# A four-layer graph network on one core: a store tied to a later sum, and second neighbour lists in layer 2

## The chip, the cores and the metric

The kernel runs on one core of a Trainium2 chip. The metric is device time in microseconds of one execution, the median over several. The engines are TensorE (PE, with its weight loads as PEld), VectorE (DVE), ScalarE (ACT), GpSimd (POOL) and SyncE (SP). SP and POOL issue DMAs, which 16 DMA engines carry out.

## The reference

A graph of 2708 nodes has a weighted adjacency matrix `adj` (symmetric in pattern, float32) and 512 features a node. Low-numbered nodes have many neighbours, high-numbered ones few. Four pre-norm layers follow one another; each adds its output to `x`:

```python
# layer 0: incidence
mask = adj > 0
head = mask / sqrt(sum(mask, -1))
inc = adj + head
x = x + (inc @ h) / sum(inc, -1)          # h = relu(layernorm(x))
# layer 1: attention, 8 heads, masked with adj
atts = q @ k.T / sqrt(64) - 1e16 * (1 - max(adj, I))
x = x + softmax(atts) @ v @ Wo
# layer 2: two graph convolutions
h = relu(adj @ (h @ W1) + b1)             # pass 1
h = relu(adj @ (h @ W3) + b3)             # pass 2
x = x + tanh(h @ Wf + bf)
# layer 3: mean over neighbours
A = (adj != 0)
x = x + (A @ (h @ W + b)) / sum(A, 0)
```

## The kernel before

The nodes are cut into 22 tiles of 128 (the last has 20). A row tile `m` is a block of 128 outputs; its product with the adjacency matrix is a sum over column tiles. Since the matrix is sparse, only the first six column tiles (`DENSE` = 6, 768 nodes) are multiplied as dense blocks. For the other columns each row tile has a list of the nodes that are a neighbour of any of its 128 nodes, in chunks of 128:

```python
CHUNKS = (0, 10, 9, 8, 7, 7, 7, 7, 6, 6, 6, 6, 6, 6, 6, 5, 6, 5, 5, 5, 5, 2)
```

Row tile 0 has no list and multiplies all tiles. For a listed chunk the kernel gathers 128 rows of features and 128 rows of the row tile's adjacency columns by indirect DMAs on POOL, one gather each.

Layer 0 builds the lists while it computes (loop at L729). The adjacency rows of a tile are loaded (L473, `ar`); ACT and PE count the neighbours by column (`counts`, stored at L277), and for a group of three row tiles (`GROUP`) a running sum gives each column its rank in the list (`rank_blocks`, L314 to L321, which stores `rank_b`; `rank_rows` for row tiles 1 and 2, which stores `rank_l` at L342). `load_ranks` (L354, L360) spreads a row's ranks over the 128 partitions, and `search` (L363 on) finds the place of each rank with a find-index operation on DVE (L377) and writes the indices `idx_a` (for adjacency entries) and `idx_g` (for feature rows). POOL then gathers the adjacency entries `ac` (L532, three buffers) and the feature rows `h` (L550). `incidence(m)` builds `inc` from dense blocks `at` (loaded at L574) and `incl` from `ac` with two DVE operations each (`add_head`, L592 and L600), PE sums them into `acc` (L741), and `ac` itself is kept for later layers: its store to `listed[m]` (`lst`, L618) is put on the list `pending`, which `flush` issues from SP at the next turn of the loop. The rest of a turn belongs to layers 0 and 1: norm, transposes (L185), value projection (L157), the store of `y` (L695), loads of `x` (L701, L705).

Layer 2's pass 1 (loop at L1039) goes over row tiles 0 to 9, 21, 10 to 20. `aggregate` (L905) loads `ac` back (L890), gathers feature rows of the first product from `g1d` (L897) into eight places `gg0` to `gg7`, and loads the six dense column tiles in two pieces of three (`raw`, L880). The dense product is exact to float32 by three reduced-precision products of split operands: `a_hi` (ACT, L933), `a_lo` and `a_s` (DVE, L934 and L935), three matmuls for each column tile (L946). The listed chunks use float32 matmuls (L949, two records each in the profile). In pass 1 (`marked`) ACT also writes the sign of every block to `nz` (L915), which is stored for layer 3. Then come the bias (L974), relu and transposes (L837 to L846), the next projection (`project3`, L862), its sum `go` (L830, L831) and its store to `g2d` (L1048). All first products (L1009 to L1025, with stores to `x2` and to `g1d`) fall into the turn of row tile 0. Pass 2 (loop at L1208: row tiles 0, 6 to 9, 21, 10 to 20, 1 to 5) is the same without marks, with gathers from `g2d`. Layer 3 (L1133 and around) counts with the marks.

The program text gives an order of issue for each engine that is then rearranged: [...] So an added dependence can change where instructions of other engines stand. Buffers are given by name in pools with a set number of copies; [...]

Of the kernel before, what the change touches and what calls it, by code (L numbers as in the profile page):

```python
# [9 lines left out]
FP = mybir.dt.float32  # L10
FR = mybir.dt.float32r
BF = mybir.dt.bfloat16
HF = mybir.dt.float16
U32 = mybir.dt.uint32
# [3 lines left out]
ALU = mybir.AluOpType  # L18
# [4 lines left out]
P = 128  # L23
# [12 lines left out]

DENSE = 6
LEAD = 3
CHUNKS = (0, 10, 9, 8, 7, 7, 7, 7, 6, 6, 6, 6, 6, 6, 6, 5, 6, 5, 5, 5, 5, 2)


@with_exitstack
def kernel(
# [27 lines left out]
    nc = tc.nc  # L71
# [15 lines left out]
    def rows(t):  # L87
        return min(P, N - t * P)

    def dense_of(m):  # L90

        return 0 if m == NT - 1 else DENSE
# [33 lines left out]
    BEHIND = DENSE * P  # L126
    WIDE, LOW = (N - BEHIND) // 4, BEHIND // 2
    assert WIDE * 4 == N - BEHIND and WIDE < BLK and LOW * 2 == BEHIND
    cnt_b = dram.tile([NGROUP, P, WIDE], BF, name="cnt_b")
    cnt_l = dram.tile([NGROUP, P, LOW], BF, name="cnt_l")  # L130

# [2 lines left out]

    idx = const.tile([P, NT], U32, name="idx")
    BAD_BOUND, BAD_NEG, BAD_MANY = NT, NT + 1, 2 * NT + 1
    bad = const.tile([P, 3 * NT + 1], FP, name="bad")
    nc.gpsimd.memset(bad, 0.0)
    flag = const.tile([P, 1], I32, name="flag")

# [1 line left out]
    idx_g = const.tile([P, NT, NCH], U32, name="idx_g")  # L142

    rdeg = const.tile([P, NT], FP, name="rdeg")
    ones_b = const.tile([P, 1], BF, name="ones_b")
    nc.gpsimd.memset(ones_b, 1.0)

# [69 lines left out]
    with tc.tile_pool(name="l0_slab", bufs=2) as slabs, tc.tile_pool(  # L217
# [29 lines left out]
        nc.gpsimd.iota(place_i, pattern=[[P, NCH]], base=1, channel_multiplier=1)  # L247
        places = hp.tile([P, NCH], FP, name="places")
        nc.vector.tensor_copy(places, place_i)

        pending, pending_c = [], []

# [329 lines left out]
        def incidence(m):  # L582

            n = rows(m)
            rn = row[m][0]
            dg = wp.tile([P, P], FP, name="dg")
            nc.vector.tensor_scalar(dg[:n, :n], ident[:n, :n], rn[:n], None, op0=ALU.mult)
            rb = ps_small.tile([P, P], FP, name="rb")
            nc.tensor.matmul(rb[:, :n], ones[:n], dg[:n, :n], start=True, stop=True)

            def add_head(inc, a, k, num):
                nc.vector.scalar_tensor_tensor(  # L592
                    inc,
                    a,
                    0.0,
                    rb[:k, :n].unsqueeze(1).to_broadcast([k, num, n]),
                    op0=ALU.is_gt,
                    op1=ALU.mult,
                )
                nc.vector.tensor_tensor(inc, inc, a, ALU.add)  # L600

            pairs = []
            if m >= LEAD:
                pieces = [tiles_d] if dense_of(m) else []
            else:
                pieces = in_order if m + 1 < LEAD else dense_last
            for ts in pieces:
                if m == 0:
                    for t in ts:
                        h0_tile(t)  # L610
                at, k = blocks.pop(m) if m in blocks else load_block(m, ts)
                d = (slice(0, k), slice(0, len(ts)), slice(0, n))
                inc = slabs.tile([P, PIECE0, P], FP, name="inc", bufs=3)
                add_head(inc[d], at[d], k, len(ts))
                pairs += [(inc[:k, i, :n], h0[t][:k]) for i, t in enumerate(ts)]
            if m >= LEAD:
                ac, gs = gathers.pop(m)
                pending.append(lambda: nc.sync.dma_start(out=listed[m], in_=ac))  # L618
                inc = slabs.tile([P, NCL, P], FP, name="incl")[:, : CHUNKS[m], :n]
                add_head(inc, ac, P, CHUNKS[m])  # L620
                pairs += [(inc[:, c, :], g) for c, g in enumerate(gs)]
            return pairs

# [189 lines left out]
    NMARK = DENSE + NCA  # L813
    gather_slot = [0]

    def gathered():
        name = f"gg{gather_slot[0] % NGG}"
        gather_slot[0] += 1
        return gp.tile([P, D], FP, name=name)

    def sum_banks(dst, main, mixed, n):

# [54 lines left out]
    def load_piece(m, ts):  # L877
        n, k = rows(m), rows(ts[0])
        raw = ap.tile([P, PIECE, P], FP, name="raw", bufs=3)
        nc.sync.dma_start(  # L880
            out=raw[:k, : len(ts), :n],
            in_=adj_t[ts[0] * P : ts[0] * P + k * len(ts), m * P : m * P + n].rearrange(
                "(t p) m -> p t m", p=k
            ),
        )
        return raw[:k, : len(ts), :n], k

    def load_listed(m):
        ac = ap.tile([P, NCA, P], FP, name="ac")[:, : CHUNKS[m], : rows(m)]
        nc.sync.dma_start(out=ac, in_=listed[m])  # L890
        return ac

    def gather(m, gd, gs=None, index=idx_g):

# [10 lines left out]
    def aggregate(m, parts, shifted, gd, marked):  # L905
# [4 lines left out]
        if marked:  # L910
            nz = ap.tile([P, NMARK, P], U8, name="nz", bufs=3)

            def mark(i, a):
                k, ts = a.shape[:2]
                nc.scalar.activation(nz[:k, i : i + ts, :n], a, AF.Sign)  # L915
# [1 line left out]
        mixed = ps_a.tile([P, D], FP, name="aggs")  # L917
        chunks = []
        if num:
            ac = load_listed(m)  # L920
            chunks = [(ac[:, c, :], g) for c, g in enumerate(gather(m, gd))]
            if marked:
                mark(whole, ac)
        for ts in dense if dense_of(m) else []:
            gs = [parts(t) for t in ts]
            raw, k = load_piece(m, ts)
            hi, lo, s = (
                ap.tile([P, PIECE, P], FR, name=f"a_{part}") for part in ("hi", "lo", "s")
            )
            d = (slice(0, k), slice(0, len(ts)), slice(0, n))  # L930
            if marked:
                mark(ts[0], raw)
            nc.scalar.activation(hi[d], raw, AF.Copy, scale=UP)  # L933
            nc.vector.tensor_tensor(lo[d], raw, hi[d].bitcast(FP), ALU.subtract)  # L934
            nc.vector.scalar_tensor_tensor(  # L935
                s[d], lo[d].bitcast(FP), SHIFT, hi[d].bitcast(FP), op0=ALU.mult, op1=ALU.add
            )
            for i, t in enumerate(ts):
                ghi, glo, gs_ = gs[i]
                first, last = t == 0, t == DENSE - 1  # L940
                for acc, a, b, st, sp in (
                    (main, hi, ghi, first, False),
                    (main, lo, glo, False, last),
                    (mixed, s, gs_, first, False),
                ):
                    nc.tensor.matmul(acc[:n], a[:k, i, :n], b[:k], start=st, stop=sp)  # L946
# [89 lines left out]
    w3 = split_w(wsetb, wr, "wb")  # L1036
    wr = load_w(wset, wf_d, "wr")

    for m in order_m:  # L1039
        n = rows(m)  # L1040
        parts = aggregated(m, first_parts, first_product, g1d, bias1, marked=True)
        if m == 0:
            wf = split_w(wset, wr, "wa")
            wr = load_w(wset, w_d, "wr")
        main, mixed = project3(parts, n, w3)
        go = wp.tile([P, D], FP, name="go")
        sum_banks_scaled(go, main, mixed, n)
        nc.sync.dma_start(out=g2d[span(m)], in_=go[:n])  # L1048
# [158 lines left out]
    FIRST = 2  # L1207
    for m in order_2:  # L1208
        n = rows(m)
        parts = aggregated(m, second_parts, second_product, g2d, bias3)  # L1210
        if m == 0:
            w = split_w(wsetb, wr, "wb")
# [499 lines left out]
```

## Time and profile before

| | |
|---|---|
| median of 9 runs | 1521.31 us (1518.84 to 1529.21) |
| profiled execution | 1525.66 us, of which its span is 1523.9 us |
| mean granted TensorE clock | 0.935 |
| HBM traffic | 230 GB/s over the span |
| layer 0 | about 60 to 520 us |
| layer 2, pass 1 | 540 to 950 us, of which row tile 0 up to about 655 us |
| layer 2, pass 2 | 960 to 1280 us |
| layer 3 | from 1280 us |

Times within a trace count from the span's start. In lines of a timeline the first number is the start, the second the duration, both in us; square brackets give the idle time of that engine just before and what ended it. `SPq` is a DMA issue on SP's queue. A line of the waits view reads: who waited, for whom, us in total, times, longest. [...]

### The profile page before, as it was taken

To read this page: it belongs to the slowest core of one execution; us is meant where nothing else is said; L and a number is where in the kernel's file an instruction comes from. 1 tells how busy PE (TensorE), PEld (TensorE's weight loads), DVE (VectorE), ACT (ScalarE), POOL (GpSimd) and SP (SyncE) were. 2 spreads that over 40 slices of the span, in tenths; PEclk is the share of its full clock that TensorE was granted. 3 is DMA by queue.
4 is the path that set the end of the run, shared out by engine and by line. 5 is a ranking of instruction groups with operands and counts; after the bars stand their busy time and mean duration, and the time that the engine had idled before them with its cause. 6 is when DMAs were issued, how large, how long until landed. Compare 5 with 4: busy or idle time off the path is not lost.

```text
span 1523.9 us, 15398 instructions
## 1 busy us (share of the span) xinstructions
PE 1313.0 (86%) x4400; PEld 772.9 (51%) x4400; DVE 940.5 (62%) x1888; ACT 676.8 (44%) x1040; POOL 673.0 (44%) x690
## 2 busy tenths in 40 slices
PE   6487689789778669979999999899999998777887
PEld 2133234334333247645656665565667666565564
DVE  3568688878879579533344445555666655564654
ACT  5987375363111256422333334444454544444443
POOL 1264566666553321055544442243343444066653
PEclk9699989899889889999999999999999999798999
DMA  8999888987696687277777777655555656476864
GB/s 307 314 328 323 286 284 298 298 272 225 192 327 216 172 282 245 93 222 252 247 234 227 235 232 245 198 183 187 157 172 176 202 185 201 155 229 208 250 209 151
DMA packets 195940, 351.27 MB, mean 231 GB/s; under 512 B 26444, under 2 KB 107692, under 8 KB 192113
## 3 DMA queue, kind: packets, MB, share of 16 engines
q1 hardware_dynamic: 148453, 200.68, 39.6%
q0 software_dynamic: 47392, 149.51, 31.5%
q8 instruction: 37, 0.61, 0.2%
q14 instruction: 58, 0.48, 0.1%
HBM read 286.99 MB, written 63.12 MB: 230 GB/s over the span
## 4 chain that ended last, share of the span: by engine, by line
PE 51%; DMA 5%; DVE 3%; issue 3%; ACT 2%; another core or an unknown queue 2%; SPq 0%; ACTq 0%; POOLq 0%; DVEq 0%; POOL 0%
PE aggs L949 13%; PE main L862 9%; PE agg L946 7%; PE mixed L862 4%; PE agg L1133 4%; PE aggs L946 4%; PE aggs L1133 3%; PE pt L837 3%; DMA raw<-in_adj_t_dram 2%; PE agg L862 1%; PE aggs L961 1%; PE mixed L1133 1%; PE main L1133 1%; DMA ac<-lst 1%
## 5 line engine op out<-in xcount | busy, mean ns | idle before, releaser
L949 PE MATMUL aggs<-gg,ac 128*128 128x512 f32 (+1 forms) x520 | 232.4, 594 | 4.5 <-DMA gg<-g1d,idx_g 3.5
L897 POOL DMA_INDIRECT gg<-g2d,idx_g x130 | 131.0, 1008 | 223.0 <-PE aggs L949 173.4
L897 POOL DMA_INDIRECT gg<-g1d,idx_g x130 | 132.4, 1019 | 181.3 <-PE aggs L949 108.4
L741 PE MATMUL acc<-h,inc 128*128 128x512 f32 x348 | 166.8, 620 | 33.2 <-DVE inc L600 27.3
L532 POOL DMA_INDIRECT ac<-in_adj_t_dram,idx_a x130 | 130.2, 1002 | 78.4 <-issue 38.1
L550 POOL DMA_INDIRECT h<-h0d,idx_g x111 | 117.7, 1060 | 103.7 <-PE acc L741 70.4
L949 PEld LDWEIGHTS aggs<-gg,ac 128*128 128x128 f32 (+1 forms) x520 | 97.5, 189 | 111.3 <-issue 103.4
L741 PEld LDWEIGHTS acc<-h,inc 128*128 128x128 f32 x348 | 65.0, 196 | 111.7 <-issue 74.1
L933 ACT ACTIVATE a_hi<-raw 128x384 fp32r<-128x384 f32 x84 | 43.5, 520 | 168.8 <-issue 96.6
L946 PE MATMUL agg<-ghi,a_hi 128*128 128x512 f32 x252 | 115.1, 457 | 3.4 <-ACT a_hi L933 3.1
L946 PE MATMUL agg<-glo,a_lo 128*128 128x512 f32 x252 | 102.4, 406 | 4.1 <-ACT glo L200 4.1
L897 POOL DMA_INDIRECT gg<-hidr,idx_h x79 | 78.2, 990 | 58.0 <-PE agg L1133 20.6
L741 PE MATMUL acc<-h,incl 128*128 128x512 f32 (+1 forms) x222 | 103.2, 611 | 0.0
L946 PE MATMUL aggs<-gs,a_s 128*128 128x512 f32 x252 | 100.4, 401 | 0.7 <-DVE gs L197 0.6
L934 DVE TENSOR_TENSOR a_lo<-raw,a_hi 128x384 fp32r<-128x384 f32 x84 | 47.2, 562 | 85.0 <-ACT a_hi L933 48.5
L157 PE MATMUL yacc<-wvo,hT 128*128 128x512 f32 (+1 forms) x176 | 88.7, 650 | 8.8 <-ACT hT L186 5.2
L843 DVE SCALAR_TENSOR_TENSOR v_lo<-pt,v_hi 128x512 fp32r<-128x512 f32 (+1 forms) x88 | 56.9, 665 | 48.3 <-ACT v_hi L842 28.6
L824 DVE SCALAR_TENSOR_TENSOR u<-aggs,u 128x512 f32<-128x512 f32 x42 | 28.9, 687 | 79.2 <-PE aggs L949 57.8
L842 ACT ACTIVATE v_hi<-pt 128x512 fp32r<-128x512 f32 (+1 forms) x88 | 49.0, 578 | 47.7 <-PE pt L837 36.4
L483 ACT ACTIVATE sgn<-ar 128x2708 bf16<-128x2708 f32 (+1 forms) x22 | 54.0, 2455 | 34.1 <-DMA ar<-in_adj_dram 28.2
L741 PEld LDWEIGHTS acc<-h,incl 128*128 128x128 f32 (+1 forms) x222 | 42.7, 196 | 52.0 <-issue 51.3
L514 DVE FIND_INDEX8 at_top<-top,ar 128x8 uint32<-128x2708 f32 (+1 forms) x22 | 65.3, 2970 | 0.0
(275 smaller groups left out, 2785.0 us busy)
## 6 DMA issues: line engine op xcount, KB each, us to landing
ar<-in_adj_dram SPq DMA_DIRECT2D x27, 1354.0 KB
raw<-in_adj_t_dram SPq DMA_DIRECT2D x108, 192.0 KB
slot<-x SPq DMA_DIRECT2D x41, 256.0 KB
at<-in_adj_t_dram SPq DMA_DIRECT2D x27, 384.0 KB
ranks<-rank_b SPq DMA_DIRECT2D x20, 485.0 KB
ac<-lst SPq DMA_DIRECT2D x16, 384.0 KB
h<-in_x_dram SPq DMA_DIRECT2D x21, 256.0 KB
h0d<-h POOLq DMA_DIRECT2D x21, 256.0 KB
```

What stands on the lines that cost most here:

```text
L157: nc.tensor.matmul(acc[:n], hT[:, c, :n], w[:, c, :], start=(c == 0), stop=(c == NCD - 1))
L483: nc.scalar.activation(sgn[:n], ar[:n], AF.Sign, accum_out=sum_sgn[:n])
L514: nc.vector.max_index(at_top[:n], top[:n], ar[:n])
L532: nc.gpsimd.indirect_dma_start(out=ac[:, c, :n], out_offset=None, in_=adj_units, in_offset=bass.IndirectOffsetOnAxis(ap=idx_a[:, m, c0 + c ...
L550: nc.gpsimd.indirect_dma_start(out=g, out_offset=None, in_=h0d[:, :], in_offset=bass.IndirectOffsetOnAxis(ap=idx_g[:, m, c : c + 1], axis=0),)
L741: nc.tensor.matmul(acc[:n], a, g, start=(i == 0), stop=(i == len(pairs) - 1))
L843: nc.vector.scalar_tensor_tensor(lo[d], pt[d], 0.0, hi[d].bitcast(FP), op0=ALU.max, op1=ALU.subtract)
L862: nc.tensor.matmul(acc[:n], a[:, c, :n], b[:, c, :], start=first and c == 0, stop=last and c == NCD - 1,)
L897: nc.gpsimd.indirect_dma_start(out=gs[c], out_offset=None, in_=gd[:, :], in_offset=bass.IndirectOffsetOnAxis(ap=index[:, m, c : c + 1], ax ...
L946: nc.tensor.matmul(acc[:n], a[:k, i, :n], b[:k], start=st, stop=sp)
L949: nc.tensor.matmul(mixed[:n], a, g, start=(c == 0 and not dense_of(m)), stop=(c == len(chunks) - 1),)
L1133: nc.tensor.matmul(bank_h(m)[: rows(m)], a, b, start=(i == 1), stop=(i == total))
```

## The change

There are two parts.

In layer 0, after the sum of a row tile's listed entries, an operation of one element writes the minimum of `ac[0,0,0]` and the sum's first element back to `ac[0,0,0]`. The sum is never below the entry, so the value stays the same; the store of `ac` now depends on the sum.

In layer 2, row tiles 12 to 20 multiply only the first two column tiles as dense blocks. For columns of tiles 2 to 5 (512 nodes) each gets a second list of two chunks. `few_ranks` makes the ranks out of the stored counts (`cnt_l`) for all nine row tiles at once and stores them (`rank_f`); `load_few_ranks` spreads a row over the partitions; `few_search` finds the indices, which go to free columns of `idx_g`; and `gather_few` gathers, in each of the two passes, two chunks of adjacency entries (64 KB each, into free columns of the `ac` tile) and two of feature rows (256 KB each). Places named `slot1` to `slot4` are added to the eight `gg` places, for row tiles 12 to 17 in pass 1 and 12 to 20 in pass 2. In pass 1 both dense pieces are still loaded and marked for layer 3; in pass 2 one piece of two tiles is loaded. A further column of `bad` notes a list that is too long for its chunks.

```diff
+SPARSE, FEW, FEW_CHUNKS = 12, 2, 2
...
                 add_head(inc, ac, P, CHUNKS[m])
+
+                nc.vector.tensor_tensor(
+                    ac[:1, 0, :1], ac[:1, 0, :1], inc[:1, 0, :1], ALU.min
+                )
...
+    more_places = [[]]
+
     def gathered():
-        name = f"gg{gather_slot[0] % NGG}"
+        names = [f"gg{i}" for i in range(NGG)] + more_places[0]
+        name = names[gather_slot[0] % len(names)]
...
+    def few_ranks():
+
+        r = NFULL - SPARSE
+        total, rank = (
+            gp.tile([P, D], FP, name=f"slot{i}").bitcast(to) for i, to in ((5, BF), (6, HF))
+        )
+        for g in range(r // GROUP):
+            nc.sync.dma_start(
...
+                in_=cnt_l[SPARSE // GROUP + g, : 2 * QUAD].rearrange("(b i) w -> i b w", b=2)[
+                    :GROUP
+                ],
+            )
+        rank = rank[:r, :BETWEEN]
+        nc.vector.tensor_scalar_min(rank, total[:r, FEW * P : DENSE * P], 1.0)
+        nc.vector.tensor_tensor_scan(rank, rank, rank, 0.0, ALU.add, ALU.max)
+        nc.sync.dma_start(out=rank_f[SPARSE:NFULL], in_=rank)
...
+    def load_few_ranks(m):
+        few[m] = gp.tile([P, D], FP, name=f"slot{7 + m - SPARSE}").bitcast(HF)
+        nc.sync.dma_start(
+            out=few[m][:, :BETWEEN], in_=rank_f[m : m + 1].to_broadcast([P, BETWEEN])
+        )
+
+    def few_search(m):
...
+        nc.vector.tensor_scalar_add(end, ranks[:, BETWEEN - 1 : BETWEEN], 1.0)
+        nc.vector.tensor_copy(ranks[:, BETWEEN:], end)
+        nc.vector.tensor_scalar(want, places_f, end, None, op0=ALU.min)
+        nc.vector.max_index(at, want, ranks)
...
     def load_listed(m):
-        ac = ap.tile([P, NCA, P], FP, name="ac")[:, : CHUNKS[m], : rows(m)]
-        nc.sync.dma_start(out=ac, in_=listed[m])
-        return ac
+        ac = ap.tile([P, NCA, P], FP, name="ac")[:, :, : rows(m)]
+        nc.sync.dma_start(out=ac[:, : CHUNKS[m]], in_=listed[m])
+        return ac[:, : CHUNKS[m]], ac[:, FEW_A : FEW_A + FEW_CHUNKS]
+
+    def gather_few(m, gd, ac):
+
+        gs = [gathered() for _ in range(FEW_CHUNKS)]
+        for dst, src, i in [(ac[:, c, :], adj_units, FEW_A + c) for c in range(FEW_CHUNKS)] + [
+            (g, gd[:, :], FEW_G + c) for c, g in enumerate(gs)
+        ]:
+            nc.gpsimd.indirect_dma_start(
...
         if num:
-            ac = load_listed(m)
+            ac, ac_few = load_listed(m)
             chunks = [(ac[:, c, :], g) for c, g in enumerate(gather(m, gd))]
             if marked:
                 mark(whole, ac)
-        for ts in dense if dense_of(m) else []:
+        taken = whole
+        if is_sparse(m):
+            taken = FEW
+            chunks += gather_few(m, gd, ac_few)
+        for ts in dense if whole else []:
+            if not marked:
+                ts = [t for t in ts if t < taken]
+                if not ts:
+                    continue
+            raw, k = load_piece(m, ts)
+            if marked:
+                mark(ts[0], raw)
+            ts = [t for t in ts if t < taken]
+            if not ts:
+                continue
+            raw = raw[:, : len(ts)]
             gs = [parts(t) for t in ts]
-            raw, k = load_piece(m, ts)
...
-    for m in order_m:
+    for i, m in enumerate(order_m):
         n = rows(m)
+
+        more_places[0] = [f"slot{i}" for i in range(1, 5)] if SPARSE <= m < NFULL - 3 else []
+        if m == SPARSE // 2 - 4:
+            few_ranks()
+        if is_sparse(m + SPARSE // 2 + 1):
+            load_few_ranks(m + SPARSE // 2 + 1)
+        if is_sparse(m + SPARSE // 2 - 1):
+            few_search(m + SPARSE // 2 - 1)
...
     for m in order_2:
         n = rows(m)
+        more_places[0] = [f"slot{i}" for i in range(1, 5)] if is_sparse(m) else []
```

## The prediction

> **What bounds the kernel now.** I read the engine totals first, then the slices, then busy time by stage, and only then the timeline of the stages that the change touches.
>
> ```profile
> PE 1313.0 (86%) x4400; PEld 772.9 (51%) x4400; DVE 940.5 (62%) x1888; ACT 676.8 (44%) x1040; POOL 673.0 (44%) x690
> PE   6487689789778669979999999899999998777887
> DMA  8999888987696687277777777655555656476864
> ```
>
> The digits are tenths busy of 38-us slices. The average of 86% hides two regimes: PE is short of work in the first thirteen slices (layer 0) and full in layer 2. The windows view (PE, PEld, DVE, ACT, POOL, clock, DMA share, GB/s) puts numbers to it:
>
> ```profile
> 60.00:520.00 460.00, 376.42 (x1015) 165.80 (x1016) 367.16 (x781) 207.93 (x273) 258.57 (x260) 0.91 0.81 271
> 640.00:680.00 40.00, 30.68 (x102) 17.54 (x102) 15.59 (x27) 12.74 (x24) 19.73 (x18) 0.93 0.68 212
> 680.00:920.00 240.00, 237.33 (x843) 146.35 (x841) 97.49 (x162) 76.46 (x143) 112.70 (x112) 1.00 0.73 235
> 960.00:1280.00 320.00, 312.50 (x1190) 206.74 (x1189) 193.68 (x360) 152.55 (x228) 127.60 (x127) 1.00 0.59 183
> ```
>
> Rows three and four are pass 1 (from its second row tile) and pass 2 of layer 2: PE is busy 98 to 99% at full clock, so matmul time removed there is time gained, as long as nothing else is as close. In layer 0, 84 us of PE's 460 are idle, and what ends those waits is DVE, behind DMAs behind SP.
>
> In layer 0 the queue of SP is in order: it issues loads and stores, and what it waits for holds everything behind it. Its waits there begin with the store that part 1 touches (first line: us in total, times, longest). The timeline shows one such wait and what it held back: SP issues nothing from 244.3 to 254.22, so rank_b goes out at 255.63, the ranks come late, DVE stands 9.25 us, PE 6.87.
>
> ```profile
> SPq L618 <- DMA ac<-in_adj_t_dram,idx_a: 52.0, 14, 9.1
> 254.22 0.32 SPq L618 DMA_DIRECT2D lst<-ac  x1
> ...
> 255.63 0.45 SPq L321 DMA_DIRECT2D rank_b<-rk  x1
> ...
> 265.19 1.15 SPq L354 DMA_DIRECT2D ranks<-rank_b  x2
> 271.64 0.15 DVE L370 TENSOR_SCALAR end<-ranks 128x1 f32<-128x1 f16 x1 [9.25 <-issue]
> 280.40 2.07 PE L741 MATMUL acc<-h,inc 128*128 128x512 f32 x2 [6.87 <-DVE inc L600]
> ```
>
> Pass 1, from the chain of waits (PE's listed chunks: two records each, so 5.15 / 6 = 0.86 us a chunk), PE's dense products (starts 0.23 apart) and POOL's gathers (1.25 apart, then idle until PE frees buffers):
>
> ```profile
> 839.78 5.15 PE aggs L949 x12
> 852.67 5.15 PE aggs L949 x12
> 851.15 0.39 PE L946 MATMUL agg<-ghi,a_hi 128*128 128x512 f32 x1
> 851.38 0.39 PE L946 MATMUL agg<-glo,a_lo 128*128 128x512 f32 x1
> 853.80 0.95 POOL L897 DMA_INDIRECT gg<-g1d,idx_g  x1 [5.28 <-PE aggs L949]
> 855.05 0.95 POOL L897 DMA_INDIRECT gg<-g1d,idx_g  x1 [0.30 <-issue]
> 844.96 0.32 SPq L890 DMA_DIRECT2D ac<-lst  x1
> 849.66 0.74 ACT L915 ACTIVATE nz<-ac 128x640 uint8<-128x640 f32 x1 [1.80 <-DMA ac<-lst]
> ```
>
> [...]
>
> **Part 1, the dependence in layer 0.** It adds 19 operations of one element. The nearest row is L370's, 0.15 us: 19 x 0.15 = 2.9 us of DVE, behind the sum that PE waits for and ahead of the next tile's work; at 80% DVE load (367 of 460 us) up to 2.9 may show, I take 0. The store of a row tile now waits for the gathers and for the sum of the listed entries (two DVE operations, L592 takes 0.95 us in its row). With the queue unchanged that would add about 2 us to each of 14 waits. [...] the planned orders of the two programs differ just there: the stores to listed stand about three stores later on SP; for two of the rank groups (those of 255 and 387 us) rank_b and the loads of ranks now come ahead of the store and of the ar load, for the group of 311 no store stands ahead, and rank_l still stands behind a store, but an older tile's. DVE's and PE's own orders hardly move in this layer.
>
> What could come back, by the PE waits behind such blocks: 7.7 us at 115 to 129 (1.99 + 5.67, slab loads behind the store of 112.44), 9.0 at 273 to 280 (2.09 + 6.87), 8.0 at 390 to 397 (4.32 + 3.67): 24.7 us. A further 7.3 at 333 and 10.5 at 451 have other causes as well (ranks and ar ahead of them), so I leave them. Where a block goes, SP's next wait is close: y's store on ACT (23.7 us in the layer), the inc buffers on DVE (20.2), xt on x (18.9). I take half, 12 us. Upper bound 28, with a share of the last two. Lower bound below nothing: a later store frees its ac buffer later (three buffers, so the gather three tiles on waits), as now 2.5 us twice; twice that is -5.
>
> **Part 2, the second lists.** Per row tile of 12 to 20 and pass it removes 4 dense tiles x 3 products x 0.227 = 2.7 us of PE and adds 2 chunks x 0.86 = 1.7, so 1.0 saved: 9.0 us a pass. On ACT and DVE one piece of a_hi, a_lo, a_s goes (0.52, 0.56, 0.55 us), off the path.
>
> Pass 1. POOL gets four more gathers a tile: 4 x 1.25 = 5.0 us, where it has 5.28 idle now. Tiles with 6 chunks (12, 13, 14, 16) then need 10 x 1.25 = 12.5 us of POOL against 12.9 - 1.0 = 11.9 of PE; those with 5 chunks 9 x 1.25 = 11.25 against 12.05 - 1.0 = 11.05. Together POOL 106.3, PE 102.9, before 4 x 12.9 + 5 x 12.05 = 111.9. The order moves four of the new gathers far ahead, which takes 5.0 from POOL. So the gain lies between 5.6 and 9.0. Against it: the few gathers write into the ac tile, behind its listed load and ACT's mark, 844.96 to 850.40, 5.4 us, and three to four other gathers (3.8 to 5.0 us) stand before them in most tiles; and DMA: now 235 GB/s x 12.9 us = 3.03 MB a tile, plus 2 x 64 + 2 x 256 KB = 3.7 MB in 11.9 us, 309 GB/s, where layer 0 shows slices of up to 328. I take 6.
>
> Pass 2. POOL's 12.5 us stand against 16.0 of PE, DMA has 183 GB/s; the raw pieces shrink by 256 KB a tile. 9.0 less something for gathers late at the start: 7, bounds 3 to 9.
>
> Searches. The order puts the minimum, the scan and six of the nine searches on DVE between the last first products of row tile 0, three after them. A search is one FIND_INDEX8 over 513 (L377: 2173 ns over 1941, so near 0.6 us) and eight small operations of about 0.1: 1.5 us, in all 13. DVE is idle some 6 of the 17 us before 647, while PE in 640 to 680 already lacks work (30.68 of 40). The store of rank_f, three groups of loads and their waits stand on SP between the g1d stores, on which the first gather (649.09) waits. I take 3 us lost, bounds 0 and 8. Layer 3 (from 1280) has no edit: 0.
>
> Sum: -12 + 3 - 6 - 7 = -22. From the profiled 1525.66 (span 1523.9 and 1.8 around it) that is 1503.7; it ran 4.35 above the median, so on the median 1521.31 - 22 = 1499.
>
> **Rivals.**
> A, the forecast: 1499; within it layer 0 may be off by 8, the searches by 4, each pass by 3, in quadrature 10: 1489 to 1509.
> B, the stalls of layer 0 only move: the block goes and y, xt or at hold SP instead; then -10 from layer 2, 1511. For it: SP's other waits total more than L618's. Against: the rank chain of 255 to 280 is freed by order, not by luck.
> C, layer 0 gives up its 28 and layer 2 its 15: -28 + 3 - 15 = -40, 1481. For it: three stalls have the same cause; against it, DMA share in the layer is 0.81, so loads issued sooner don't all land sooner.
> D, slower: POOL blocks in pass 1. If the ac gather waits with one gather ahead instead of four (the order for tiles 18 to 20), POOL stands 5.4 - 1.25 = 4.2 us in each tile, and it has no slack left. 9 x 4.2 = 38 us more: 1499 + 38 = 1537. It turns the whole to slower from 22 / 9 = 2.4 us a tile. [...] against it: most tiles have more ahead, and the load of ac goes out a tile and a half before use.
> E, nothing: layer 0 at 0 and PE's saving eaten by POOL and the searches, -0 to -3: 1520.
>
> **How the numbers follow.** A 0.45, B 0.18, C 0.10, D 0.20, E 0.07. The predicted time is A's. Range 1479 to 1532: C in it, and D up to a block of 3.6 us a tile; the rest is left out. A measurement here tells 0.2% (3 us) from none. Faster: A, B, C less a tail of B, 0.71; same: E and that tail, 0.08; slower: D and the far end of E, 0.21.
>
> **What would show it.** Part 1: L618's waits on SP far under 52 us, and DVE's first wait for ranks (9.25 at 271) gone; if their sum moves to L695, L701 or L574, it is B. Part 2: row tile periods of about 12 us (6 chunks) in pass 1 and 15 in pass 2, L946 shrunk by 216 matmuls over both passes, L949 at 0.86 a chunk; POOL idle near zero in 820 to 920. If PE waits there for gg or ac, with POOL waiting for ACT's mark, it is D. The prediction is wrong if row tile 0 ends over 8 us later, or if layer 0 gets longer: then the moved stores delay something that I took to be slack.

## The result, and the profile after

The changed kernel takes 1570.27 us (median of 10, 1557.04 to 1578.11), the kernel before in the same measurement 1520.82 (31 runs): a ratio of 1.0316, with a 95% interval from 1.0293 to 1.0340. It is slower, by 48 us going by the ratio. The profiled run took 1570.37 us, its span is 1568.6. The forecast was 1499, and the range up to 1532 does not hold the result.

The engine totals and slices of the page after:

```profile
PE 1312.4 (84%) x4256; PEld 752.9 (48%) x4256; DVE 935.6 (60%) x1964; ACT 665.5 (42%) x1022; POOL 746.0 (48%) x762
PE   6489778789987499879998788998988998677987
DMA  8899798787893884667787777665665665377774
```

PE has 144 matmul records fewer than before and is busy for the same time (1313.0 then): the work shrank, but parts of it ran at a lower clock (0.95 in 680 to 920 and 0.98 in 960 to 1280, where both had 1.00). The row of nines in layer 2 is gone. By stage, in the same windows and columns as before (PE, PEld, DVE, ACT, POOL, clock, DMA share, GB/s):

```profile
60.00:520.00 460.00, 380.89 (x1024) 165.95 (x1024) 369.67 (x805) 210.84 (x279) 264.47 (x261) 0.92 0.82 271
640.00:680.00 40.00, 26.45 (x79) 15.55 (x78) 20.06 (x59) 10.11 (x19) 23.43 (x22) 0.83 0.69 224
680.00:920.00 240.00, 218.12 (x718) 130.46 (x717) 85.69 (x143) 69.77 (x132) 126.77 (x128) 0.95 0.73 229
960.00:1280.00 320.00, 291.90 (x1026) 177.72 (x1025) 167.18 (x312) 132.31 (x199) 149.35 (x152) 0.98 0.62 192
```

In pass 1 PE lacks work for 21.9 of 240 us where it lacked 2.7, and its clock fell to 0.95. In pass 2 it lacks 28.1 of 320 where it lacked 7.5. POOL is far from full in both (127 of 240, 149 of 320), and DMA moves about what it moved. So no engine has become the bound by its total; PE waits for single results.

To place the time I cut the span at four records of PE. Row tile 0 runs from the last product of layer 0 to the first listed product of layer 2, pass 1 from there to the first dense product of pass 2, pass 2 to its last listed product. These are single profiled executions, in us:

| kernel | layer 0 ends | row tile 0 | pass 1 | pass 2 | layer 3 |
|---|---|---|---|---|---|
| before | 507.5 | 150.2 | 280.3 | 357.3 | 228.7 |
| after | 498.0 | 154.4 | 308.9 | 377.4 | 229.8 |
| difference | -9.5 | +4.2 | +28.6 | +20.1 | +1.1 |

They sum to +44.5, and the spans differ by 44.7. Layer 0 gained nearly what was forecast; both passes lost.

Where single row tiles of a pass are timed below, a row tile runs from the start of the sum `u` on DVE (L913, before the bias) of the row tile before it to its own. A projection that is late in row tile 13 by this count is that of row tile 12, which follows its sum.

The waits of PE, first in 680 to 920 and then in 960 to 1280 (us in total, times, longest):

```profile
PE main L951 <- ACT v_hi L931: 17.8, 3, 6.2
...
PE main L951 <- issue: 10.2, 10, 3.3
PE agg L1061 <- ACT a_hi L1048: 4.0, 1, 4.0
```

Pass 1 has three waits of some 6 us, at the first product of the projection (`project3`, L862 before, L951 now). The timeline around the first one, in row tile 13 (`remote` means that the view finds no instruction that ended the wait):

```profile
835.04 0.63 PE L926 MATMUL pt<-ident,u 128*128 128x128 f32 x4 [1.12 <-DVE u L1089]
...
837.59 0.94 POOL L988 DMA_INDIRECT ac<-in_adj_t_dram,idx_g  x1 [0.30 <-issue]
838.84 0.94 POOL L988 DMA_INDIRECT ac<-in_adj_t_dram,idx_g  x1 [0.31 <-issue]
841.56 0.94 POOL L1000 DMA_INDIRECT gg<-g1d,idx_g  x1 [1.78 <-issue]
842.06 0.60 ACT L931 ACTIVATE v_hi<-pt 128x512 fp32r<-128x512 f32 x1 [3.74 <-remote]
842.71 2.07 PE L951 MATMUL main<-wb,v_hi 128*128 128x512 f32 x4 [6.18 <-ACT v_hi L931]
...
856.34 1.19 PE L951 MATMUL main<-wb,v_hi 128*128 128x512 f32 x4
```

The transposes that `v_hi` needs are recorded as ended at 835.67. ACT stands idle for 3.74 us before it reads them at 842.06; in the next row tile, without a stall, it read them 0.10 us after their recorded end (854.99 + 0.60 to 855.69). Then the four products take 2.07 us where they take 1.19 at 856.34: the clock has halved. The granted clock is 1.00 in 836 to 840, 0.54 in 840 to 844, 0.61 in 844 to 848 and 1.00 in 848 to 852; behind the other two waits it is 0.50 in 876 to 880 and in 908 to 912. A wait of some 6 us thus costs some 2 to 3 us more behind it: row tiles 13, 15 and 17 are 7.9, 8.6 and 8.4 us longer than undisturbed ones, and 6.2, 6.2 and 5.4 of that are the wait.

The counter that PE raises for ACT tells where the lateness lies. In the trace's record of semaphores it goes up at 842.03, and ACT starts 0.03 us later. So ACT takes the result up at once; what is late is PE's product or PE's signal of it.

The few gathers do not wait for their tile's load or mark: in both passes each of the 36 gathers of adjacency entries starts 0.30 or 0.31 us after the one before it. And POOL made 17 gathers from 817.36 to 838.84 without a longer pause than 1.3 us. The kernel before has one wait that looks the same, a sign that the profile before had to offer: after 17 gathers from 653 to 674 us PE stands for 4.4 us in row tile 2 of pass 1.

```profile
676.37 0.52 ACT L933 ACTIVATE a_hi<-raw 128x384 fp32r<-128x384 f32 x1 [18.89 <-remote]
677.79 1.89 PE L862 MATMUL main<-wb,v_hi 128*128 128x512 f32 x4 [4.38 <-ACT v_hi L842]
```

### The profile page after: what moved, and what is told of

It reads as the page before. It is cut to its first block, busy times and chain, and to the rows that moved or that the text cites. A ratio compares the mean times of both kernels' runs of the same rounds, so it can differ in the third digit from the quotient of the medians.

```text
span 1568.6 us, 15346 instructions
## 1 busy us (share of the span) xinstructions
PE 1312.4 (84%) x4256; PEld 752.9 (48%) x4256; DVE 935.6 (60%) x1964; ACT 665.5 (42%) x1022; POOL 746.0 (48%) x762
## 4 chain that ended last, share of the span: by engine, by line
PE 44%; issue 7%; DMA 5%; DVE 4%; ACT 2%; another core or an unknown queue 2%; SPq 0%; DVEq 0%; POOLq 0%; ACTq 0%; POOL 0%
PE aggs L1064 13%; PE main L951 8%; PE agg L1061 4%; PE mixed L951 4%; PE agg L1256 3%; PE aggs L1061 2%; PE pt L926 2%; PE aggs L1256 2%; DMA raw<-in_adj_t_dram 2%; PE aggs L1076 1%; PE main L1256 1%; PE agg L951 1%; PE mixed L1256 1%; DVE gg L1198 1%
## 5 line engine op out<-in xcount | busy, mean ns | idle before, releaser
L539 POOL DMA_INDIRECT ac<-in_adj_t_dram,idx_a x130 | 139.4, 1072 | 104.5 <-issue 32.6
L1000 POOL DMA_INDIRECT gg<-g1d,idx_g x119 | 118.7, 997 | 147.0 <-PE aggs L1064 67.7
L1000 POOL DMA_INDIRECT gg<-g2d,idx_g x111 | 109.2, 984 | 165.5 <-PE aggs L1064 117.2
L752 PE MATMUL acc<-h,inc 128*128 128x512 f32 x348 | 162.4, 608 | 15.7 <-DVE inc L607 9.8
L1048 ACT ACTIVATE a_hi<-raw 128x384 fp32r<-128x384 f32 (+1 forms) x66 | 32.3, 491 | 173.7 <-issue 81.8
L1061 PE MATMUL agg<-ghi,a_hi 128*128 128x512 f32 x180 | 84.4, 469 | 7.4 <-ACT a_hi L1048 4.0
L951 PE MATMUL main<-wb,v_hi 128*128 128x512 f32 (+1 forms) x176 | 58.2, 456 | 33.1 <-ACT v_hi L931 25.9
L163 PEld LDWEIGHTS yacc<-wvo,hT 128*128 128x128 f32 (+1 forms) x176 | 35.7, 212 | 83.9 <-issue 55.5
L1061 PE MATMUL agg<-glo,a_lo 128*128 128x512 f32 x180 | 73.2, 407 | 0.1
L913 DVE SCALAR_TENSOR_TENSOR u<-aggs,u 128x512 f32<-128x512 f32 x42 | 28.9, 687 | 74.0 <-PE aggs L1064 49.2
L1049 DVE TENSOR_TENSOR a_lo<-raw,a_hi 128x384 fp32r<-128x384 f32 (+1 forms) x66 | 34.6, 524 | 64.0 <-ACT a_hi L1048 33.2
L1061 PE MATMUL aggs<-gs,a_s 128*128 128x512 f32 x180 | 71.4, 406 | 1.2 <-issue 0.7
```

Of the source, the lines that this page charges most:

```text
L163: nc.tensor.matmul(acc[:n], hT[:, c, :n], w[:, c, :], start=(c == 0), stop=(c == NCD - 1))
L539: nc.gpsimd.indirect_dma_start(out=ac[:, c, :n], out_offset=None, in_=adj_units, in_offset=bass.IndirectOffsetOnAxis(ap=idx_a[:, m, c0 + c ...
L752: nc.tensor.matmul(acc[:n], a, g, start=(i == 0), stop=(i == len(pairs) - 1))
L951: nc.tensor.matmul(acc[:n], a[:, c, :n], b[:, c, :], start=first and c == 0, stop=last and c == NCD - 1,)
L1000: nc.gpsimd.indirect_dma_start(out=gs[c], out_offset=None, in_=gd[:, :], in_offset=bass.IndirectOffsetOnAxis(ap=index[:, m, c : c + 1], ax ...
```

## The experiments

All stage times below are of one profiled execution each. Ratios are against the kernel before, in the same measurement. The first four runs take the change apart.

**Part 1 alone**: the kernel before with only this.

```diff
                 add_head(inc, ac, P, CHUNKS[m])
+                nc.vector.tensor_tensor(
+                    ac[:1, 0, :1], ac[:1, 0, :1], inc[:1, 0, :1], ALU.min
+                )
```

> Part 1 alone: the kernel before with the one-element operation after the sum of the listed entries, and nothing of the second lists. In the changed kernel the last product of layer 0 starts at 498.0 us where it was 507.5. If part 1 is the cause of that, this kernel is about 9 us faster than before (near 1511 us), all of it before 510 us. If the shorter layer 0 came from the new plan that the second lists brought about, the time stays near 1521 us.

1503.09 us (4 runs, 1492.04 to 1513.69), ratio 0.9873 (0.9819 to 0.9928). Layer 0 ends at 497.6, the passes take 281.0 and 355.9, as before. Part 1 is a gain by itself, and this kernel beats both. Its profiled execution, 1513.69, is the longest of the four, so its stages may be some us long.

**Part 2 alone**: the changed kernel without that operation.

```diff
-                nc.vector.tensor_tensor(
-                    ac[:1, 0, :1], ac[:1, 0, :1], inc[:1, 0, :1], ALU.min
-                )
```

> Part 2 alone: the changed kernel without the one-element operation. If the two parts simply add up, layer 0 is as before, and the time is the changed kernel's plus 9: near 1579 us, slower than before by some 58 us. If part 1 itself does harm further on (an ac tile or a store late in layer 2), this kernel is faster than the changed one, under 1570 us.

1573.37 us, ratio 1.0342 (1.0286 to 1.0398). Layer 0 ends at 520.4, row tile 0 takes 143.6, the passes 305.5 and 372.8. The loss is all of part 2. Beside part 2 the new store order is worth little: this median lies 3 us above that of the changed kernel. Layer 0 is 22.4 us longer here, but row tile 0 is 10.8 shorter.

**The second lists in one pass each.**

```diff
-        if is_sparse(m):
+        if is_sparse(m) and not marked:
             taken = FEW
```

This is the edit for pass 2; for pass 1 it reads `and marked`. The other pass is also without the four added places. Ranks and searches stay in both.

> The changed kernel with the second lists in pass 2 only; pass 1 multiplies six dense tiles everywhere, as before. By the changed kernel's trace pass 1 lost 28.6 us and pass 2 20.2 us. If the two losses are independent, this one ends near 1570 - 29 = 1541 us, and its pass 2 (from the first product of row tile 0 to the end of the last listed chunk) is again about 20 us longer than before. If pass 2 is slow only as a result of what pass 1 leaves behind (late g2d rows, places still taken), its pass 2 is as before, 357 us, and the time near 1520 us.

> The changed kernel with the second lists in pass 1 only; pass 2 multiplies six dense tiles everywhere. If the losses are independent, it ends near 1570 - 20 = 1550 us, with three stalls of some 6 us of PE in pass 1 followed by half clock, as in the changed kernel. If the stalls in pass 1 come from the work for pass 2 that the new plan puts in front on ScalarE (the early splitting of g2 rows), they are fewer here, and the time is well under 1545 us.

In pass 2 only: 1534.68 us, ratio 1.0117 (1.0072 to 1.0162), passes 280.8 and 377.8. In pass 1 only: 1532.34, ratio 1.0066 (1.0027 to 1.0104), passes 307.3 and 354.1. Each pass shows its own loss, whole, with or without the other: two independent losses, 26.3 and 21.9 us beside part 1 alone. In pass 1 long row tiles come again, 13, 15, 16 and 17 (20.1, 15.9, 18.2 and 15.7 us), with waits of PE of 3.3 to 6.1 us.

The next four keep or drop parts of a second list.

**Only the removal**: the second lists' gathers and products left out.

```diff
             taken = FEW
-            chunks += gather_few(m, gd, ac_few)
```

> The changed kernel without the second lists' gathers and products: row tiles 12 to 20 multiply two dense tiles and their own list, and the neighbours in tiles 2 to 5 are left out of the sum (their ranks and indices are still made). Two theories for the +28 us of pass 1 and the +20 of pass 2. Supply: four more gathers a row tile on POOL (1.25 us each) and their landing are what PE waits for; without them PE is the bound again and each pass loses its 9 x 2.7 = 24.5 us of dense products: pass 1 near 281 - 24 = 257 us, pass 2 near 356 - 24 = 332 us, in all near 1460 us. Cover: the twelve dense products were what PE did while ScalarE and VectorE made the parts for the next projection; with six there is nothing to do in that time, whatever is gathered: pass 1 stays over 275 us and pass 2 over 350 us, in all over 1495 us.

1499.48 us, ratio 0.9871 (0.9819 to 0.9924); passes 270.1 and 351.4. Beside part 1 alone, 216 dense products of 0.227 us are gone, 49.0 us of PE; pass 1 is shorter by 10.9 and pass 2 by 4.5. So most of what was removed had not set the time, even with nothing put in its place. In row tiles 12 to 20 by themselves 17.0 and 7.0 of 24.5 us come back; in pass 1 row tiles 1 and 2, in pass 2 row tiles 1 to 5 are longer (more on both below).

**Only the gathers**: they are made, and the dense products stay.

```diff
-            taken = FEW
-            chunks += gather_few(m, gd, ac_few)
+            gather_few(m, gd, ac_few)
```

> The changed kernel with all six dense tiles multiplied; the four new gathers of a row tile and pass are issued, and no product reads what they bring. Supply: the own list's gathers still stand in one queue with the new ones, 10 x 1.25 = 12.5 us a row tile against some 12.9 of PE; passes of over 290 and over 365 us, in all over 1530 us. Cover: PE has its filling back, passes near 281 and 356 us, in all near 1510 us.

1529.58 us, ratio 1.0087 (1.0039 to 1.0136); passes 293.4 and 365.0, so 12.4 and 9.1 more than with part 1 alone, with PE's work unchanged. One row tile of pass 1 stands out, 15 with 18.2 us beside 12.0; PE waits there for 3.6 us.

**Both**: gathers, their products and the dense products.

```diff
-            taken = FEW
             chunks += gather_few(m, gd, ac_few)
```

> The changed kernel with all six dense tiles multiplied and the second lists as well (the neighbours in tiles 2 to 5 are summed twice), so that PE has 1.7 us more a row tile and pass than in the kernel before and 2.7 more than in the changed one. Cover: PE is the bound, passes near 281 + 15 = 296 and 356 + 15 = 371 us, in all near 1540 us: faster than the changed kernel with more work. Supply: not faster than the changed kernel, passes of 309 and 377 us or more, in all 1570 us or more.

1546.05 us (2 runs), ratio 1.0180 (1.0117 to 1.0242); passes 306.0 and 385.1. PE has 49 us more to do than in the changed kernel, and the median is 24 us lower. But this is no measure of the stalls: layer 0 is 14.5 us shorter here, which is spread between executions (see layer 0 below), and layer 3 15.1, though the edit is in layer 2 alone. Pass 1 is 2.9 us shorter with 24.5 us more work on PE, and pass 2 is 7.7 longer. What the run shows of pass 1: its row tiles 12 to 20 are even, 13.6 to 16.3 us, and PE waits nowhere in them for over 1.5 us.

What goes with the stalls of pass 1 is the longest row of gathers in row tiles 12 to 20, counted without a fill or a pause over 1.35 us in it:

| kernel | longest rows | longest waits of PE there, us |
|---|---|---|
| after | 19, 18 | 6.2, 6.2 |
| part 2 alone | 18, 17 | 5.4, 5.2 |
| in pass 1 only | 18 | 6.1 |
| last three row tiles (below) | 16 | 3.8 |
| only the gathers | 15 | 3.6 |
| both, and with pauses (below) | 10 | under 3 |
| no adjacency gathers (below) | 8 | under 3 |
| only the removal | 8 | 3.1 |
| no new gathers (below) | 6 | 1.0 |

Waits of the second kind, told of further on, are left out. The run in pass 1 only has two more waits, of 4.5 and 4.2 us, after rows of 10 and 8 with a pause of 1.57 us between them, and the 3.1 us of the removal came with no new gather, so no sharp limit can be read from this.

**No gathers of adjacency entries**: half of the new gathers.

```diff
-        for dst, src, i in [(ac[:, c, :], adj_units, FEW_A + c) for c in range(FEW_CHUNKS)] + [
+        for dst, src, i in [
             (g, gd[:, :], FEW_G + c) for c, g in enumerate(gs)
...
-            chunks += gather_few(m, gd, ac_few)
+            chunks += gather_few(m, gd, ac)
```

> The changed kernel without the two adjacency gathers of a row tile and pass: the second list's products take the first two chunks of the own list's adjacency entries instead (the sum is of other entries, the work on PE the same). POOL then has 8 gathers where it had 10, 10.0 us against 11.9 of PE. Supply, by the number of gathers: PE the bound again, passes near 281 - 9 = 272 and 356 - 9 = 347 us, in all near 1490 us. Cover, or the landing of the row gathers alone: as the changed kernel, 309 and 377 us, in all near 1570 us.

1533.83 us, ratio 1.0095 (1.0068 to 1.0121); passes 293.8 and 364.5. Two gathers fewer a tile give back 15 and 13 us; rival D's place, the gather behind the mark, could not give anything in pass 2, where nothing is marked. One long wait is left, at row tile 17 (6.9 us, of the second kind).

**Gathers beside a chain that needs nothing from them.** A program of its own, without the network: PE and ACT pass one result back and forth, and POOL issues rows of 40 gathers: alone, beside loads, and beside loads with four fills after every sixth gather.

> A kernel of its own that leaves out the whole network and stores rows of a mean: TensorE and ScalarE pass one tile to and fro (a float32 product of 128x512, a copy), some 1.5 us a turn, while POOL issues three runs of 40 gathers of 256 KB: from turn 20 on with nothing else, from turn 100 on beside SP's loads of 192 KB, from turn 200 on beside such loads and with four fills of a tile on POOL after every sixth gather. In the changed kernel the results of PE reach ScalarE late (5 to 6 us) at the end of unbroken rows of gathers. If the row itself is the cause, the turns get longer after 15 to 20 gathers in the first two runs (2 us and more), and stay at 1.5 us in the third. If it takes the loads as well, only in the second. If the lateness has another cause in the full kernel (a wait on a landing that the profile does not show), no turn is longer than some 1.7 us anywhere.

One run, 1243.74 us. A turn takes 2.76 us, longer than I had expected, and three turns out of all are late: one at the end of the first row, two at the end of the second, none in the row with fills. The timeline at the end of the first row:

```profile
107.71 0.95 POOL L93 DMA_INDIRECT gg<-in_x_dram,idx  x1 [0.30 <-issue]
107.83 0.60 ACT L136 ACTIVATE v<-acc 128x512 f32<-128x512 f32 x1 [2.16 <-PE acc L135]
108.47 2.07 PE L135 MATMUL acc<-v,mean 128*128 128x512 f32 x2 [0.69 <-issue]
108.96 0.95 POOL L93 DMA_INDIRECT gg<-in_x_dram,idx  x1 [0.31 <-issue]
112.57 0.60 ACT L136 ACTIVATE v<-acc 128x512 f32<-128x512 f32 x1 [4.15 <-remote]
```

ACT's other waits are 2.16; this one is 4.15, with the same sign ("remote") as in the stalls of pass 1. The counter that PE raises goes up at 112.55 here, and ACT starts 0.02 later. The effect is there without shared data, without loads, and it goes with the row of gathers: DMA's share is 0.71, 0.98 and 0.95 over the three rows, so a full DMA is neither needed for it nor enough; but it came after some 35 to 40 of them and was 2.0, 2.0 and 2.8 us, later and smaller than I had expected.

**Only the last three row tiles** (18 to 20) with second lists.

```diff
-SPARSE, FEW, FEW_CHUNKS = 12, 2, 2
+SPARSE, FEW, FEW_CHUNKS = 18, 2, 2
```

> The changed kernel with the second lists for row tiles 18 to 20 only (SPARSE 18 in the place of 12); with part 1. In the changed kernel's pass 1 row tile 18 takes 10.7 us where part 1 alone takes 12.0. If three tiles are few enough for POOL, they save 1.2 us each in both passes, less 1 to 3 us for the three searches: 1503 - 5 = 1498 us. If the second lists cost something wherever they are (a later start of the gathers, the plan of pass 2), it is over 1508 us.

1536.89 us (20 runs) beside 1527.49 before, ratio 1.0062 (1.0035 to 1.0089). The expectation missed: not even a third of the lists is free. The passes take 286.5 and 367.0; single row tiles stand out (19 with 15.75 us in pass 1, 17 and 18 with 19.1 and 23.95 in pass 2). The profiled execution, 1525.96, lies 11 us below the median, so these stages don't hold the whole loss.

**Pauses**: the changed kernel with four more operations on POOL in each tile, before the gathers of a second list (the place is overwritten by its gather).

```diff
         gs = [gathered() for _ in range(FEW_CHUNKS)]
+        for _ in range(4):
+            nc.gpsimd.memset(gs[0], 0.0)
```

> The changed kernel with four fills of a place on POOL (some 0.54 us each in the kernel that ran gathers alone, 2.2 us together) among the gathers of each second list, so that no row of gathers stays unbroken for long; POOL has 2.2 us more a row tile. Late results at the end of unbroken rows: the three stalls of 6 to 7 us in row tiles 13, 15 and 17 of pass 1 go, POOL is the bound with 4 x 14.7 + 5 x 13.5 = 126 us for the nine row tiles where the changed kernel took 134, and pass 1 takes near 300 us (308.9 in the changed kernel). Number of gathers alone (POOL's time, or their landing): 9 x 2.2 = 20 us longer, near 329 us, with the stalls where they were.

1535.87 us, ratio 1.0084 (1.0032 to 1.0136): 34 us faster than the changed kernel, with 72 more operations on the very engine that the forecast feared for. The trace shows the fills between the gathers (two at 817.15, one each at 819.39 and 821.04), and by the traces PE, ACT, DVE and SP carry out the same instructions in the same order as in the changed kernel; only POOL's order differs. Pass 1 takes 298.1, pass 2 362.8. The windows view of this kernel for 680 to 920:

```profile
680.00:920.00 240.00, 223.41 (x749) 132.14 (x748) 89.55 (x149) 72.41 (x137) 147.50 (x164) 0.97 0.76 238
```

And PE's long waits in the same stretch, from its waits view:

```profile
PE main L951 <- ACT v_hi L931: 8.2, 1, 8.2
```

POOL is busy for 147.5 us instead of 126.8, and two of the three waits are gone. The one left, at row tile 17, is of another kind (below).

**No new gathers at all**: in their place the own list's first two chunks are multiplied a second time.

```diff
-            chunks += gather_few(m, gd, ac_few)
+            chunks += chunks[:FEW_CHUNKS]
```

> The changed kernel without the second lists' gathers; in their products' place PE multiplies the own list's first two chunks once more (other entries are summed, the work of PE is that of the changed kernel, POOL's that of the kernel before). Against part 1 alone this is PE's 1.0 us less a row tile and pass and nothing more on POOL. If PE's work were the bound, pass 1 takes 281 + 4 - 9 = 276 us (4 for the searches ahead of row tile 1) and pass 2 356 - 9 = 347 us. Cover: with six dense products in place of eighteen PE waits for ScalarE and VectorE in part of each row tile: pass 1 over 281 us, pass 2 over 358 us. What is left up to the changed kernel's 308.9 and 377.4 us is the gathers' own.

1524.75 us (20 runs), ratio 0.9991 (0.9966 to 1.0015). Its profiled execution took 1534.62, so up to 10 us of its stages may not be the kernel's; they are 283.9 and 363.2, and layer 0, with the changed kernel's text, ends 9.1 us later than there.

These runs form a ladder from part 1 to the whole change:

| step | change of the median, us | pass 1 | pass 2 | work by the count |
|---|---|---|---|---|
| dense products gone (part 1 alone to only the removal) | -3.6 | -10.9 | -4.5 | 216 x 0.227 = 49.0 us less on PE |
| listed products added (to no new gathers) | +25.3 | +13.8 | +11.8 | 36 x 0.86 = 31.0 us more on PE |
| gathers added (to after) | +45.5 | +25.0 | +14.2 | 72 x 1.25 = 90 us more on POOL |

The medians are from four measurements, with 1518.96 to 1522.53 for the kernel before; by the ratios the steps are -0.3, +18 and +49 us, so single us of them are not sure. The last two rows of the passes have the uncertainty of the run without gathers. In row tiles 12 to 20 alone the steps are -17.0, +15.6 and +23.6 in pass 1 and -7.0, +5.6 and +13.7 in pass 2.

**The second kind of stall.** The third long wait of the changed kernel, in row tile 17, has another cause:

```profile
896.46 3.41 SPq L1182 DMA_DIRECT2D slot<-g2d  x4
...
903.22 0.63 ACT L196 ACTIVATE ghi<-slot 128x512 fp32r<-128x512 f32 x1 [4.30 <-DMA slot<-g2d]
...
905.32 0.58 ACT L931 ACTIVATE v_hi<-pt 128x512 fp32r<-128x512 f32 x1
...
905.96 2.07 PE L951 MATMUL main<-wb,v_hi 128*128 128x512 f32 x4 [5.42 <-ACT v_hi L931]
```

Row tiles 12 to 20 no longer read the parts of g's column tiles 2 to 5, so their places come free earlier. The splitting of `g2` for pass 2 (`ghi`), which ran on ACT at 919 to 927 us in the kernel before, at the end of pass 1, has one step at 816 here and three at 903 to 908, three row tiles before the end; where the dense products of pass 1 stay (the runs with lists in pass 2 only, with only the gathers, and with both), all stand at the end of the pass as before. On ACT it now stands ahead of `v_hi` and waits for a load. The run without adjacency gathers has the same wait at the same row tile (20.4 us for that tile), as the waits view of its ACT shows:

```profile
ACT ghi L196 <- DMA slot<-g2d: 9.3, 2, 6.8
```

Part of that line is the row tile's; the runs with pauses (9.0) and without gathers (5.9) have it too. In the run without gathers PE stands for 6.2 us behind it, so this stall needs no new gather: row tiles 16 and 17 take 18.03 and 12.48 us there. No run took this wait away by itself, so its price, some 6 to 8 us with the half clock behind it (0.50 in 908 to 912), is read from traces only.

**Pass 2.** No wait of PE in 960 to 1280 is over 4.0 us, but there are many. A projection, in the changed kernel:

```profile
1129.04 1.07 PE L951 MATMUL mixed<-wb,v_s 128*128 128x512 f32 x4
1131.29 1.19 PE L951 MATMUL main<-wa,v_hi 128*128 128x512 f32 x4 [1.17 <-ACT go L912]
```

PE waits for ACT's sum. In the kernel before, the next tile's eighteen dense products are laid between such steps, and PE waits at `main` for 1.8 us in all from 960 to 1280; now six are left to lay there, and it waits for 14.5 (10.2 of `issue`, 3.6 and 0.7 of ACT).

## Why the prediction was wrong

- **Layer 0, -12**: right in direction and cause. -9.5 in the changed kernel, -9.9 with part 1 alone. The waits of SP for the gathered entries, 52.0 us in 14, have become waits for the tied operation. From the waits view of the changed kernel, SP's queue:

```profile
SPq L712 <- DMA x<-xt: 36.9, 7, 10.0
...
SPq L625 <- DVE ac L629: 10.4, 2, 6.1
```

  Part of it moved, as rival B had it, to a load of `x` that waits for a store from the same place (18.9 before). The size is loosely determined: in the kernels with both parts, the end of layer 0 lies between 482 and 507 us, although by the traces each engine carries out the same instructions of layer 0 there in the same order (but for one or two on POOL and PE at its end). So this is a spread of single executions, and that -9.5 came so near to -12 is in part luck. By the ratio, part 1 alone gains 19 us (11 to 28).
- **Searches, +3**: right for row tile 0 (+4.2). But row tiles 1 and 2 take 6.5 us more than with part 1 alone (25.94 and 23.27 beside 21.78 and 20.91). The searches by themselves are not the cause: with lists in pass 2 only, all nine are made and the two tiles take 43.0 together, as with part 1 alone (42.7). What the longer runs share is the four added places (`slot1` to `slot4`) in pass 1: the kernels without them there (before, part 1 alone, pass 2 only, last three) take 42.7 to 43.4 us, all others 46.8 to 49.5, with or without new gathers, with or without the dense products. How the places do it was not taken apart; the forecast has no term for them.
- **Pass 1, -6: this step failed, measured +28.6.** 6.5 of it are those of row tiles 1 and 2, some 22 stand in row tiles 12 to 20. Three terms, against part 1 alone. First, "PE is busy 98 to 99% at full clock, so matmul time removed there is time gained": of 24.5 us of dense products removed, 10.9 came back, or 17.0 in row tiles 12 to 20 by themselves. Second, the listed products cost 13.8 of their 15.5 (15.6 in row tiles 12 to 20), near the price, but by some luck: the run without gathers holds a stall of the second kind, the one before it other waits of up to 3.1 us. Third, the gathers were priced as throughput: POOL's 12.5 us a tile against PE's 11.9, so at most 9.0 - 5.6 = 3.4 us. They cost 25.0 (23.6 in row tiles 12 to 20). The term left out that after an unbroken row of gathers PE's results come late. It also put at nothing the places that come free earlier, which brought the second kind of stall. The saving itself is there where nothing stalls: undisturbed row tiles of six chunks take 11.59 us beside 12.9, those of five 10.74 beside 12.05. Three tiles of 19.47, 19.30 and 19.11 eat it.
- **Pass 2, -7: this step failed too, measured +20.1.** "POOL's 12.5 us stand against 16.0 of PE" is true and did not help: the gathers cost 14.2 there as well, and of 24.5 us of removed dense products only 4.5 came back, since they had been the work that covered ACT and DVE between projections. The forecast named no cover for this edit. One place of it: row tile 3 of pass 2 takes 23.3 us beside 18.3 with part 1 alone; it is as long with nothing gathered anew (23.2 with only the removal, 24.4 without gathers) and 18.6 to 19.7 in the four other kernels where the dense products of pass 2 stay, so it goes with the removed products and not with the gathers.
- **Layer 3, 0**: right (+1.1).
- **Rival D, 1537**, had the place and nearly the size of pass 1 right (38 beside 28.6), missed pass 2, and had the mechanism wrong: the few gathers never wait for a mark, and without them pass 2, where there is no mark, gives back nearly as much as pass 1.

What the runs show of the cause: the gathers' rows, not their sum. More work on POOL that breaks the rows, with every other engine's order unchanged, takes 34 us off, of it 10.8 in pass 1 and 14.6 in pass 2 (pauses). In pass 1, 24.5 us more work on PE with rows of at most 10 gathers leave the pass no longer (both), and a chain that shares no data with the gathers is late at the end of a row (the program of its own). Whether it is the number in a row or the rate of the gathers that counts is not separated.

Why PE's result comes late after such a row is open. In the program of its own the product is recorded as ended at 110.54, and the counter goes up at 112.55. Whether the product or its signal was late, no run here shows. POOL pauses as well (1.78 us before 841.56) and DMA's share falls to 0.28 in 840 to 844, but neither speaks strongly against a fault of PE alone, since gathers too wait for PE's products to free their places (1.29 us before the one at 862.73).

A rival that no run excludes is the recording itself, as every run here was recorded. In the program of its own the views find what ended each of ACT's waits between the rows; within the rows they often do not (`issue`): for 10 of 18 waits in the first row, 13 of 17 in the second, 5 of 23 in the row with fills. ACT's waits in the first row, 60 to 110 us:

```profile
ACT v L136 <- issue: 21.6, 10, 2.2
ACT v L136 <- PE acc L135: 16.4, 8, 2.2
```

So what ended ACT's wait is found least often where long rows stand, and it is open whether the delay is as large, or there at all, without recording.

## What to carry to other kernels

Here a busy share of 98 to 99% on TensorE did not make every product there worth its duration (of 24.5 us removed in each pass 10.9 and 4.5 came back): ask of each group that is removed which waits of other engines it covers, and look at what stands between the steps of the next dependent chain. Do not price added gathers by their sum alone (in pass 1 at most 3.4 us by the sum, 25.0 measured); look at the longest stretch in which GpSimd issues without a pause, and where it grows, leave gaps (34 us here) or try a version with less of it first. Measure the two parts of a change apart: here one operation of one element was worth 1.3%, and the large edit beside it hid that.

## What had not been expected of the hardware

- In these recorded runs, after long rows of gathers at 1.25 us each, PE's results reach ScalarE 2 to 6 us late: 6 us in pass 1 after 17 gathers, 2.0 to 2.8 us in the program of its own after 35 to 40. Extra GpSimd work between the gathers makes the kernel 34 us faster.
- A late result cost twice here, once as the wait (6.18 us) and once by the clock: granted 0.54 in 840 to 844, with 2.07 us for four products that take 1.19 at a clock of 1.00 (856 to 860).
- In these traces a gather holds GpSimd for 0.95 us and the next follows 0.30 later, whether it moves 64 KB (`ac`) or 256 KB (`gg`).
